# A four-layer graph network on one core: attention rows ahead of copies, a bias added in pieces, and the order of work at the changes of layer

## The chip, the cores and the metric

The kernel runs on one core of a Trainium2 chip. Its engines are named as in the profile: PE (TensorE, matrix products; PEld is its weight load), DVE (VectorE), ACT (ScalarE), POOL (GpSimd) and SP (SyncE, which issues the transfers). Each engine has one queue and works it off in order. The metric is the time of one execution on the device, in microseconds (us), and the median over runs is compared. The clock that PE was granted is given as a share of full speed.

## The reference

The input is `x` [32, 512, 128] (32 batches of 512 nodes with 128 features, f32) and one adjacency matrix `adj` [512, 512] with positive weights where there is an edge. Four layers follow, each of the form x = x + layer(h) with h = relu(layernorm(x)):

- layer 0: A is a softmax over the rows of a score matrix that stands only on the edges; out = diag(A) h W0 + (A without its diagonal) h W1 + bias
- layer 1: the polynomials x1 = adj^T h and x2 = 2 adj^T x1 - h, and then relu([h, x1, x2, x1, x2] Theta + bias); the kernel has x2 from one matrix ("cheb", 2 adj adj - 1) that is made once
- layer 2: f = relu(h psi + psi_b); m = (adj*adj)^T f; out = relu([m, h] phi1 + phi1_b) phi2 + phi2_b
- layer 3: scores (h q)(h k)^T / sqrt(128), then 8 tanh(./8), exp, a mask by adj, rows divided by their sum, and the product with h and v

## The kernel before

**Pairs and stages.** The 32 batches are worked on in 16 pairs, q = 0 to 15; a pair's `x` stays in SBUF as `xt[q]`, 128 partitions by 1024 elements, from its load to its store. Each layer is a generator (`layer0` to `layer3`), whose `yield`s cut it into stages. At the end of the kernel a loop with the lists `waiting` and `active` runs them: in each step it starts the generators of one entry of `waiting`, and takes every active one to its next `yield`. So layer 1 of pair 15 and layer 2 of pair 0 are active together, and so on. After the prologue a scheduler orders the instructions of each engine from the sequence in which they were written; an instruction that is wrapped in `keep_in_program_order` is not moved ahead of what is written before it.

**The prologue** (up to line 614) is written in the order in which it is to run. It makes the attention matrix of layer 0 in four row blocks: `score_rows` on PE, `softmax_rows` (L553 to L557, DVE and ACT), `scaled_rows` (L561 to L566; ACT multiplies, POOL takes the diagonal off), and `transpose_rows` (L403, PE), whose four banks `p_attT` are copied to `attT` at L598. In between stand the pieces of work of the first pairs: `normal` (relu and normalising, L216 on ACT), `turned` (PE transposes L248 and the copy L251 on ACT), `project` (p_g, L365, and its copy L397), and `pieces[i]`, the rows of the cheb matrix (L414). `p_adiag` (L606) and layer 0's products `p_l` wait for the whole of `attT`.

**Products by seven.** Products with the 512x512 matrices are made for two batches together with seven products of half-size blocks instead of eight (`mixed` and `products`, L299 to L350). Their right sides come from `right_blocks`: four POOL operations, L290 to L293, named rt_h or rt_feat. The results gather in the PSUM banks a, c and d, in the sequence

```
ORDER = ((1, "a", True), (6, "c", True), (5, "d", True), (7, "c", False), (2, "a", False),
         (4, "c", False), (3, "d", False))
```

Between two products in bank c, DVE takes the first one out: L332 evicts product 6, and product 7 then goes on in the same bank.

**Layer 1** ends with L709 (y on DVE) and L710, x = max(y, 0) + x, which has two inputs in SBUF. **Layer 2** evicts f on DVE (L723) and takes its relu on ACT (L724), makes rt_feat on POOL, forms msgT (L312), adds phi2_b to the whole pair in one POOL operation (L730), goes through phi1 (L735, L736) and phi2, and adds the result to x (L741). `ln_stats` then has the statistics of the next layer: L194 (DVE), L200 (ACT), L203 and L205 (DVE). **Layer 3** normalises on DVE with eight operations of 128x128 (L229, SBUF to SBUF), turns h with DVE's 32x32 transposes (L258, hb) and a bounce through DRAM, makes scores (L765), tanh (L766) and exp (L768) on ACT, the mask in turns on DVE and POOL (L770), av (L777), the sum into x (L782), and stores 256 KB for each batch (L784).

Of the kernel before, what the change touches and what calls it, by code (L numbers as in the profile page):

```python
# [15 lines left out]
P = 128  # L16
# [8 lines left out]
def kernel(  # L25
# [37 lines left out]
    nc = tc.nc  # L63
    B, N, D = x.shape
# [41 lines left out]
    xt = []  # L106
# [17 lines left out]
    def spread(w, n):  # L124
        return w[:, None, :].to_broadcast([P, n, D])
# [274 lines left out]
    def transpose_rows(banks, src, t):  # L400

        for j in range(NT):
            nc.tensor.transpose(banks[j][:, blk(t)], src[:, t, blk(j)], ident)  # L403
# [156 lines left out]
    def scaled_rows(t, u):  # L560
        nc.vector.reciprocal(total[:, t : t + 1], total[:, t : t + 1])  # L561
        nc.scalar.mul(split(att[:, t, :]), crossed(u), total[:, t : t + 1])
        own = split(att[:, t, :])[:, :, t, :]
        d = diag[:, t, :].rearrange("p (b c) -> p b c", c=QR)
        nc.gpsimd.tensor_mul(d, own, ident.rearrange("p (b c) -> p b c", c=QR))
        nc.gpsimd.tensor_sub(own, own, d)  # L566
# [8 lines left out]
    pt = [bank(f"p_attT_{j}") for j in range(NT)]  # L575
    us = []
    for t in range(NT):
        if t == NT - 1:
            next(project[0], None)
        us.append(softmax_rows(t))  # L580
        if t == 0:
            next(ln[1], None)
        else:
            scaled_rows(t - 1, us[t - 1])
        for _ in range(3):
            next(normal[1], None)
    scaled_rows(NT - 1, us[-1])
    next(turned[1])
    for t in range(NT):
        transpose_rows(pt, att, t)  # L590
    next(turned[1], None)
    nc.scalar.copy(qk, p[:, :D])
    rights = {0: right_of(0)}
    next(project[1])
    for q in (2, 3):
        next(ln[q])
    for j in range(NT):
        (nc.vector.tensor_copy if j % 2 else nc.scalar.copy)(attT[:, j, :], pt[j])  # L598
    next(project[1], None)
    for _ in sum_steps(attT, "att", nc.vector):  # L600
        pass
# [6 lines left out]
    for q in (2, 3):  # L608
        next(ln[q])
        next(ln[q], None)  # L610
    for i in (2, 3):
        for _ in pieces[i]:
            pass
    by_source.__exit__(None, None, None)


# [75 lines left out]
    def layer1(q):  # L692
        h = normed(q)
        yield
        hT = transposed(h, f"hT1_{q}")
        right = right_blocks(lambda J, b: h[:, b, 2 * J : 2 * J + 2, :], f"h_{q}", [nc.gpsimd] * 4)
        yield
        x1T = pair_tile(f"x1T_{q}").rearrange("p (b w) -> p b w", b=2)
        x2T = pair_tile(f"x2T_{q}").rearrange("p (b w) -> p b w", b=2)
        mixes = (mixed(f"x1T_{q}", sums["adj"], right, x1T), mixed(f"x2T_{q}", sums["cheb"], right, x2T))  # L700
        for _ in zip(*mixes):
            pass
        hs = [straight(hT, b, None, f"hs_{q}_{b}") for b in range(2)]
        yield
        for b in range(2):
            po = projected(f"p_l1_{q}_{b}", (columns(hs[b]), th[:, 0, :]), (columns(x1T[:, b]), th12[:, 0, :]),
                           (columns(x2T[:, b]), th12[:, 1, :]))
            y = late.tile([P, NT, D], F32, tag="y", name=f"y1_{q}_{b}", bufs=2)
            nc.vector.tensor_add(y, po, spread(b1, NT))  # L709
            nc.vector.scalar_tensor_tensor(xt[q][:, b], y, 0.0, xt[q][:, b], OP.max, OP.add)  # L710
        ln_stats(q)

    def layer2(q):
        h = normed(q)
        yield
        hT = transposed(h, f"hT2_{q}")
        yield
        yield
        feat = []
        for b in range(2):  # L720
            pf = projected(f"p_feat_{q}_{b}", (at(hT, b), psi))
            feat.append(late.tile([P, NT, D], F32, tag="y", name=f"feat_{q}_{b}", bufs=2))
            nc.vector.tensor_add(feat[b], pf, spread(psib, NT))  # L723
            nc.scalar.activation(feat[b], feat[b], AF.Relu)  # L724
        yield
        right = right_blocks(lambda J, b: feat[b][:, 2 * J : 2 * J + 2, :], f"feat_{q}", [nc.gpsimd] * 4)
        msgT = pair_tile(f"msgT_{q}").rearrange("p (b w) -> p b w", b=2)
        for _ in mixed(f"msgT_{q}", sums["sq"], right, msgT):
            pass
        nc.gpsimd.tensor_add(xt[q], xt[q], phi2b[:, None, None, :].to_broadcast([P, 2, NT, D]))  # L730
        yield
        h1T = pair_tile(f"h1T_{q}").rearrange("p (b w) -> p b w", b=2)
        for b in range(2):
            ph = bank(f"p_phi1_{q}_{b}")
            nc.tensor.matmul(ph, phi1[:, 1, :], hT[:, :, b, :], start=True, stop=False)  # L735
            nc.tensor.matmul(ph, phi1[:, 0, :], msgT[:, b], start=False, stop=True)  # L736
            nc.scalar.activation(crossed(h1T[:, b]), split(ph), AF.Relu, bias=phi1b)  # L737
        yield
        for b in range(2):
            po = projected(f"p_l2_{q}_{b}", (columns(h1T[:, b]), phi2))  # L740
            nc.vector.tensor_add(xt[q][:, b], po, xt[q][:, b])  # L741
        ln_stats(q)

    def layer3(q):
        h = normed(q, on_act=False)
        yield
        hT = transposed(h, f"hT3_{q}")
        yield
        yield
        for b in range(2):  # L750
            pp = bank(f"p_qkh_{q}_{b}")
            nc.tensor.matmul(pp, qk, hT[:, :, b, :], start=True, stop=True)  # L752
            both = work.tile([P, 2 * N + 2 * NT], F32, tag="pair", name=f"qkh_hv_{q}_{b}", bufs=5)
            qkh = both[:, :N]
            nc.vector.tensor_copy(crossed(qkh), split(pp))

            pv = projected(f"p_hv_{q}_{b}", (at(hT, b), vw))
            hv = both[:, N : N + NT * (D + 1)].rearrange("p (t f) -> p t f", f=D + 1)
            nc.gpsimd.memset(hv[:, :, D : D + 1], 1.0)
            nc.vector.tensor_copy(hv[:, :, :D], pv)  # L760
            yield
            ex = square_tile(f"ex_{q}_{b}")
            for t in range(NT):
                ps = bank(f"p_score_{q}_{b}_{t}")
                nc.tensor.matmul(ps, hT[:, t, b, :], qkh, start=True, stop=True)  # L765
                nc.scalar.activation(ex[:, t, :], ps, AF.Tanh, scale=1.0 / (8.0 * math.sqrt(D)))  # L766
            for t in range(NT):
                nc.scalar.activation(ex[:, t, :], ex[:, t, :], AF.Exp, scale=8.0)  # L768
                eng = nc.gpsimd if t % 2 else nc.vector
                eng.tensor_mul(ex[:, t, :], ex[:, t, :], adjTx[0][:, t, :])  # L770
            yield
            rsum = stats.tile([P, NT], F32, tag="rsum", name=f"rsum_{q}_{b}", bufs=4)
            for i0 in range(0, NT, 2):
                po = bank(f"p_av_{q}_{b}_{i0}").rearrange("p (i f) -> p i f", i=2)
                for i in range(2):
                    for t in range(NT):
                        nc.tensor.matmul(po[:, i, : D + 1], ex[:, t, blk(i0 + i)], hv[:, t, :],  # L777
                                         start=(t == 0), stop=(t == NT - 1))
                nc.vector.reciprocal(rsum[:, i0 : i0 + 2], po[:, :, D])
                for i in range(2):  # L780
                    xi = xt[q][:, b, i0 + i, :]
                    nc.vector.scalar_tensor_tensor(xi, po[:, i, :D], rsum[:, i0 + i : i0 + i + 1], xi,  # L782
                                                   OP.mult, OP.add)
            nc.sync.dma_start(out[2 * q + b].rearrange("(t p) f -> p t f", p=P), xt[q][:, b])  # L784

    adjTx = []

    def square():

        sq = square_tile("sq")  # L790
        load_crossed(sq, adj)
        adjTx.append(square_tile("adjTx"))
        load_crossed(adjTx[0], adjT_d)
        yield
        for i in range(NT):
            s = late.tile([P, N], F32, tag="hs", name=f"sq_{i}", bufs=2)
            nc.gpsimd.tensor_mul(split(s), crossed(sq[:, i, :]), crossed(sq[:, i, :]))
            nc.gpsimd.tensor_copy(sq[:, i, :], s)
        yield from sum_steps(sq, "sq")
# [10 lines left out]
    for q in range(2, NQ):  # L810
        waiting[max(q - 4, 0)].append(first[q])
    waiting[3].append(late_sums())
    waiting += [[layer1(q)] for q in range(NQ)]
    waiting[NQ + 6].append(square())
    for layer in (layer2, layer3):
        waiting += [[layer(q)] for q in range(NQ)]
    active = []
    while waiting or active:
        if waiting:
            active += waiting.pop(0)  # L820
        active = [g for g in active if next(g, active) is not active]


# [30 lines left out]
```

## Time and profile before

The median of three runs is 998.81 us (998.48 to 999.64). The profiled execution has a span of 998.5 us at a mean granted clock of 0.993.

| engine | busy us | share |
|---|---|---|
| PE | 976.4 | 98% |
| DVE | 630.4 | 63% |
| ACT | 440.9 | 44% |
| POOL | 395.1 | 40% |

PE's waits lie at these places:

| us | what PE waits for | idle us |
|---|---|---|
| 0 to 5 | the transfer of adj | 4.2 |
| 34 to 38 | transposes of h and the attention rows, prologue | 2.1, 0.3 |
| 456 | L332 late in layer 1 | 1.8 |
| 490 to 496 | L724, first pair of layer 2 | 3.5, 0.5 |
| 550 | L332 in layer 2 | 1.3 |
| 987 to 990 | L770 of the last pair | 0.9, 0.4 |

The busy time of an engine is summed over stages with different limits. PE's is so near the span that the rows of this table, with the times at which its clock falls, tell more than the busy times. In a line of a timeline, the start comes first, then the duration, engine, line, operation, out<-in, the tile's shape, the number of instructions, and in brackets how long the engine was idle before it and what released it. A group's duration runs from the start of its first to the end of its last instruction, and matmuls overlap, so that consecutive ones start before their forerunner ends.

### The profile page before, as it was taken

Reading aid. Unit: us, or ns where it says so; the run is one execution under the profiler, and the core shown is the slowest. Engines: PE = TensorE matmul, PEld = TensorE weight load, DVE = VectorE, ACT = ScalarE, POOL = GpSimd, SP = SyncE. Lnnn points to the kernel's source line nnn. Section 1 sums busy time; section 2 is a strip of 40 time slices with the busy share of each in tenths; the row PEclk is TensorE's granted clock in tenths of the full one; section 3 lists DMA queues with packets and bytes.
Section 4 is the critical chain, followed back from the end, with each engine's and each line's share of the span. In section 5 each row is a group of like instructions: output and inputs, shape, how many; then the busy total and the mean of one; then the engine's idle time right before and its main releaser. Section 6 shows DMA issues by size and latency. Waiting matters only on the chain.

```text
span 998.5 us, 16127 instructions
## 1 busy us (share of the span) xinstructions
PE 976.4 (98%) x5918; PEld 809.4 (81%) x5918; DVE 630.4 (63%) x1520; ACT 440.9 (44%) x967; POOL 395.1 (40%) x478
## 2 busy tenths in 40 slices
PE   8999999999999999999899999999999999999997
PEld 4699999989999999998777777777667777767776
DVE  8678787655555655558667888777754444444443
ACT  4863537112322323237566343333464455544452
POOL 2579998841217213136455112222132333222332
PEclk9999999999999999999899999999999999999999
DMA  9256644412131222215333344322222121211111
GB/s 254 85 134 179 179 125 130 106 52 76 43 85 43 64 64 54 73 44 140 93 94 106 102 121 122 90 71 78 69 70 74 43 74 53 72 55 54 53 30 35
DMA packets 83007, 87.17 MB, mean 87 GB/s; under 512 B 6768, under 2 KB 73072, under 8 KB 82928
## 3 DMA queue, kind: packets, MB, share of 16 engines
q1 hardware_dynamic: 82928, 86.14, 30.7%
q8 instruction: 47, 0.77, 0.3%
q14 instruction: 32, 0.26, 0.1%
HBM read 44.70 MB, written 41.42 MB: 86 GB/s over the span
## 4 chain that ended last, share of the span: by engine, by line
PE 88%; DVE 6%; ACT 2%; DMA 1%; issue 1%; POOL 1%; SPq 1%; POOLq 0%; DVEq 0%; ACTq 0%
PE p_av L777 11%; PE p_score L765 10%; PE p_l L365 10%; PE p_msgT_c L312 4%; PE p_l_c L319 4%; PE p_x1T_c L312 4%; PE p_x2T_c L312 4%; PE p_hv L365 3%; PE p_g L365 3%; PE p_msgT_a L312 3%; PE p_x1T_a L312 3%; PE p_x1T_d L312 3%; PE p_x2T_a L312 3%; PE p_x2T_d L312 3%; PE p_qkh L752 3%; PE p_l_d L319 3%
## 5 line engine op out<-in xcount | busy, mean ns | idle before, releaser
L216 ACT ACTIVATE h<-x,sh,rs 128x128 f32<-128x128 f32 x384 | 154.5, 482 | 58.4 <-PE p_x2T_d L312 46.0
L770 POOL TENSOR_TENSOR ex<-ex,adjTx 128x512 f32<-128x512 f32 x64 | 83.3, 1303 | 200.3 <-issue 147.7
L777 PEld LDWEIGHTS p_av<-qkh_hv,ex 128*128 128x128 f32 x1024 | 120.3, 193 | 11.6 <-issue 6.9
L766 ACT ACTIVATE ex<-p_score 128x512 f32<-128x512 f32 x128 | 71.8, 587 | 130.6 <-issue 112.9
L777 PE MATMUL p_av<-qkh_hv,ex 128*128 128x129 f32 x1024 | 122.9, 277 | 2.2 <-POOL ex L770 1.4
L765 PE MATMUL p_score<-qkh_hv,hT 128*128 128x512 f32 x256 | 115.1, 592 | 0.0
L258 DVE STREAM_TRANSPOSE hb_hT<-h 128x512 f32<-128x512 f32 x122 | 84.8, 701 | 24.5 <-ACT h L216 23.9
L194 DVE BATCH_NORM_STATS2 bn<-x 128x6 f32<-128x256 f32 x256 | 95.1, 419 | 1.9
L770 DVE TENSOR_TENSOR ex<-ex,adjTx 128x512 f32<-128x512 f32 x64 | 45.9, 717 | 76.1 <-ACT ex L768 76.1
L765 PEld LDWEIGHTS p_score<-qkh_hv,hT 128*128 128x128 f32 x256 | 46.2, 190 | 46.4 <-issue 44.2
L768 ACT ACTIVATE ex<-ex 128x512 f32<-128x512 f32 x128 | 76.5, 630 | 1.9
L290 POOL TENSOR_TENSOR rt_h<-h 128x256 f32<-128x256 f32 x16 | 11.6, 727 | 133.9 <-PE p_x2T_c L312 133.1
L290 POOL TENSOR_TENSOR rt_feat<-feat,feat 128x256 f32<-128x256 f32 x16 | 11.6, 726 | 126.3 <-ACT feat L724 126.3
L730 POOL TENSOR_TENSOR x<-x,phi2b 128x1024 f32<-128x1024 f32 x16 | 38.0, 2375 | 33.2 <-ACT h L216 33.2
L365 PE MATMUL p_l<-th,x2T 128*128 128x128 f32 x256 | 49.5, 275 | 0.0
L365 PE MATMUL p_l<-th,x1T 128*128 128x128 f32 x256 | 49.5, 275 | 0.0
L365 PE MATMUL p_l<-th,hs 128*128 128x128 f32 x256 | 49.5, 275 | 0.0
L397 ACT COPY g<-p_g 128x512 f32<-128x512 f32 x32 | 18.3, 579 | 62.4 <-PE p_g L365 62.3
L365 PEld LDWEIGHTS p_hv<-vw,hT 128*128 128x128 f32 x256 | 33.6, 192 | 14.9 <-issue 7.9
L634 POOL TENSOR_TENSOR hd<-hT,adiag 128x512 f32<-128x512 f32 x32 | 40.3, 1273 | 7.1 <-PE p_l_e L655 2.5
L737 ACT ACTIVATE h1T<-p_phi,phi1b 128x512 f32<-128x512 f32 x32 | 21.9, 686 | 44.9 <-PE p_phi L736 44.9
L365 PEld LDWEIGHTS p_l<-th,hs 128*128 128x128 f32 x256 | 40.1, 192 | 0.8
(229 smaller groups left out, 2181.0 us busy)
## 6 DMA issues: line engine op xcount, KB each, us to landing
d_hT<-hb_hT SPq DMA_DIRECT2D x244, 128.0 KB
hT<-d_hT SPq DMA_DIRECT2D x61, 512.0 KB
x<-in_x_dram SPq DMA_DIRECT2D x32, 256.0 KB
out_dram<-x SPq DMA_DIRECT2D x32, 256.0 KB
adj_s<-in_adj_dram SPq DMA_DIRECT2D x4, 256.0 KB
adjT_d<-adjT SPq DMA_DIRECT2D x1, 1024.0 KB
sq<-in_adj_dram SPq DMA_DIRECT2D x4, 256.0 KB
adjTx<-adjT_d SPq DMA_DIRECT2D x4, 256.0 KB
```

The lines of the kernel that those rows point to most:

```text
L194: ins = nc.vector.bn_stats(st[:, k].rearrange("p e s -> p (e s)"), xt[q][:, b, t : t + 2, :].rearrange("p t f -> p f t"))
L216: nc.scalar.activation(h[:, b, t, :], xt[q][:, b, t, :], AF.Relu, bias=shift[q][:, i : i + 1], scale=scale[q][:, i : i + 1])
L258: nc.vector.transpose(hb[:, :, b].rearrange("p j t r -> p t j r"), h[:, b].rearrange("p t (j c) -> p t j c", c=QR))
L312: nc.tensor.matmul(p[:, :H], b[:, k, :], a[:, k, :], start=(first and k == 0), stop=(k == 1), skip_group_check=True)
L319: nc.tensor.matmul(p[:, i * D : (i + 1) * D], a[:, k, blk(i)], b[:, k, :], start=(first and i == 0 and k == 0), stop=(k == 1), skip_group_ ...
L365: nc.tensor.matmul(p[:, blk(t)], hT(t), w, start=(i == 0), stop=(i == len(terms) - 1))
L634: nc.gpsimd.tensor_mul(split(s), src, split(scale))
L765: nc.tensor.matmul(ps, hT[:, t, b, :], qkh, start=True, stop=True)
L766: nc.scalar.activation(ex[:, t, :], ps, AF.Tanh, scale=1.0 / (8.0 * math.sqrt(D)))
L768: nc.scalar.activation(ex[:, t, :], ex[:, t, :], AF.Exp, scale=8.0)
L770: eng.tensor_mul(ex[:, t, :], ex[:, t, :], adjTx[0][:, t, :])
L777: nc.tensor.matmul(po[:, i, : D + 1], ex[:, t, blk(i0 + i)], hv[:, t, :], start=(t == 0), stop=(t == NT - 1))
```

## The change

Four things are changed:

1. In the prologue, two of pair 1's relu operations instead of three follow each softmax row on ACT, none follows the last, and the copies of p_g come after the last softmax. The transposes of attention rows 0 and 1 and one row of cheb are put on PE ahead of rows 2 and 3, and pair 1's h is turned later. The aim is that PE has work while the last rows of the softmax are made.
2. phi2_b is added in four POOL operations of 128x256 per pair, each held to program order, instead of one of 128x1024. It is to keep POOL from doing it early, and to have it hold what it shares with others for less time at once.
3. `layer1(0)` starts in the step of the last pair of layer 0, and `layer2(0)` in that of the last pair of layer 1, ahead of it in the list; all later pairs follow one step sooner. `square()`, which makes adj*adj, keeps its place relative to layer 1. The first pair of a layer is to be ready when the last of the layer before is done.
4. When only two generators are left, the list is turned round once, so that the last scores of pair 15 come ahead of the last av of pair 14; and the last batch is stored in two halves.

```diff
     for t in range(NT):
-        if t == NT - 1:
-            next(project[0], None)
         us.append(softmax_rows(t))
         if t == 0:
             next(ln[1], None)
         else:
             scaled_rows(t - 1, us[t - 1])
-        for _ in range(3):
-            next(normal[1], None)
+        if t < NT - 1:
+            for _ in range(2):
+                next(normal[1])
+        if t == 2:
+            transpose_rows(pt, att, 0)
+            transpose_rows(pt, att, 1)
+            next(pieces[2])
+            next(pieces[2])
     scaled_rows(NT - 1, us[-1])
+    next(project[0], None)
+    for _ in normal[1]:
+        pass
+    transpose_rows(pt, att, 2)
+    transpose_rows(pt, att, 3)
     next(turned[1])
-    for t in range(NT):
-        transpose_rows(pt, att, t)
-    next(turned[1], None)
-    nc.scalar.copy(qk, p[:, :D])
     rights = {0: right_of(0)}
-    next(project[1])
...
         (nc.vector.tensor_copy if j % 2 else nc.scalar.copy)(attT[:, j, :], pt[j])
+    next(turned[1], None)
+    next(project[1])
+    nc.scalar.copy(qk, p[:, :D])
+    next(pieces[2], None)
     next(project[1], None)
...
-        nc.gpsimd.tensor_add(xt[q], xt[q], phi2b[:, None, None, :].to_broadcast([P, 2, NT, D]))
+        for b in range(2):
+            for i in range(0, NT, 2):
+                xi = xt[q][:, b, i : i + 2, :]
+                tc.keep_in_program_order(nc.gpsimd.tensor_add(xi, xi, spread(phi2b, 2)))
...
+                if b == 1 and q == NQ - 1:
+                    nc.sync.dma_start(out_r[:, i0 : i0 + 2, :], xt[q][:, b, i0 : i0 + 2, :])
+            if not (b == 1 and q == NQ - 1):
+                nc.sync.dma_start(out_r, xt[q][:, b])
...
-    waiting += [[layer1(q)] for q in range(NQ)]
-    waiting[NQ + 6].append(square())
-    for layer in (layer2, layer3):
-        waiting += [[layer(q)] for q in range(NQ)]
+
+    waiting[-1].insert(0, layer1(0))
+    waiting += [[layer1(q)] for q in range(1, NQ)]
+    waiting[NQ + 5].append(square())
+    waiting[-1].insert(0, layer2(0))
+    waiting += [[layer2(q)] for q in range(1, NQ)]
+    waiting += [[layer3(q)] for q in range(NQ)]
     active = []
     while waiting or active:
         if waiting:
             active += waiting.pop(0)
+        if not waiting and len(active) == 2:
+            active.reverse()
         active = [g for g in active if next(g, active) is not active]
```

## The prediction

> **What bounds the kernel now.** I read the page's busy times and slices first, to know the bounding engine, and then TensorE's list of waits and the timelines round each wait.
>
> ```profile
> PE 976.4 (98%) x5918; PEld 809.4 (81%) x5918; DVE 630.4 (63%) x1520; ACT 440.9 (44%) x967; POOL 395.1 (40%) x478
> PEclk9999999999999999999899999999999999999999
> ```
>
> TensorE (PE) is busy for 976.4 of 998.5 us, so only about 22 us are idle and a shorter time must come out of these, or out of stretches at a lower clock. The one 8 in the clock row is a slice near 490 us. The waits of PE, as total, number, longest:
>
> ```profile
> PE p_msgT_a L312 <- ACT feat L724: 3.5, 1, 3.5
> PE p_attT L403 <- ACT hT L251: 2.1, 1, 2.1
> PE p_x1T_c L312 <- DVE u_x1T L332: 1.8, 1, 1.8
> PE p_msgT_c L312 <- DVE u_msgT L332: 1.5, 2, 1.3
> PE p_av L777 <- POOL ex L770: 1.4, 2, 0.9
> ```
>
> Each happens once or twice, at a change of stage. Two cost more than their length, as the timeline of PE shows (start, duration, then the wait in brackets):
>
> ```profile
> 36.54 0.66 PE L403 MATMUL p_attT<-ident,att 128*128 128x128 f32 x4 [2.10 <-ACT hT L251]
> 37.98 3.25 PE L365 MATMUL p_g<-w,hT 128*128 128x128 f32 x16
> ...
> 487.62 1.95 PE L365 MATMUL p_feat<-psi,hT 128*128 128x128 f32 x16
> 493.08 2.07 PE L312 MATMUL p_msgT_a<-sq,feat 128*128 128x256 f32 x4 [3.51 <-ACT feat L724]
> ...
> 990.20 4.14 PE L777 MATMUL p_av<-qkh_hv,ex 128*128 128x129 f32 x20 [0.42 <-POOL ex L770]
> ```
>
> Sixteen 128x128 products take 1.95 us at 487.62 and 3.25 at 37.98; the same form at 695.26 takes 1.03 for what takes 2.07 at 493.08. After a gap PE runs for some us at half rate.
>
> In the steady part of layer 2 the queue of PE has no gap at all: from 682 to 708 us it is busy 26.0 of 26.0. What DVE and POOL do there decides what an added POOL operation costs:
>
> ```profile
> 693.91 0.73 POOL L293 TENSOR_TENSOR rt_feat<-feat,rt_feat 128x256 f32<-128x256 f32 x1
> 694.89 0.17 DVE L205 SCALAR_TENSOR_TENSOR sh<-bn,rs 128x8 f32<-128x8 f32 x1
> 695.10 2.14 DVE L229 TENSOR_SCALAR h<-x,rs,sh 128x128 f32<-128x128 f32 x8
> 697.16 0.70 DVE L258 STREAM_TRANSPOSE hb_hT<-h 128x512 f32<-128x512 f32 x1
> 697.78 0.38 DVE L332 TENSOR_TENSOR u_msgT<-p_msgT_c,u_msgT 128x256 f32<-128x256 f32 x1
> 698.28 1.08 PE L312 MATMUL p_msgT_c<-sq,rt_feat 128*128 128x256 f32 x4
> ```
>
> L332 empties the bank that the next c product fills. It ends at 698.16 and the product starts at 698.28: no slack.
>
> **What the Trainium skill says.** "SBUF — State Buffer", section "Who interferes with whom": VectorE and GpSimd share a port pair as an exclusive lock; a VectorE operation with two SBUF inputs, or one in a two-port mode, contends with a GpSimd operation that reads SBUF, and whichever issues first blocks the other fully. "VectorE: DVE Perf Modes", section "What auto-detection actually checks": a single-source operation from SBUF to SBUF can enter a two-port mode; L229 is of that kind. The trace agrees on both. L710, with two SBUF inputs, takes 0.65 us alone and 2.32 behind L730; L229, whose starts are otherwise 0.26 apart, takes 1.35:
>
> ```profile
> 448.83 2.36 POOL L730 TENSOR_TENSOR x<-x,phi2b 128x1024 f32<-128x1024 f32 x1 [0.46 <-ACT h L216]
> 449.42 2.32 DVE L710 SCALAR_TENSOR_TENSOR x<-y,x 128x512 f32<-128x512 f32 x1
> ...
> 546.22 2.36 POOL L730 TENSOR_TENSOR x<-x,phi2b 128x1024 f32<-128x1024 f32 x1
> 547.32 1.35 DVE L229 TENSOR_SCALAR h<-x,rs,sh 128x128 f32<-128x128 f32 x1
> ```
>
> "TensorE: Matmul & The Clock Gate", section "Part 1: The HAM clock gate (the "warmup" mystery)", has the clock fall to half after an idle window of about 3.4 us. The trace shows the half rate, but here a gap of 2.10 was enough once, while the one of 1.80 at 456 us was not.
>
> **The change part by part.**
>
> *Prologue.* Gone are the 2.10 and 0.29 gaps, and with them the half rate: p_g loses 3.25 - 1.95 = 1.3 to it, p_adiag (1.43 us) about 0.5. Together 4.2. The chebyshev row that now runs between the attention transposes (half of the 7.03 us of the two rows at 42.29) fills the time in which the last softmax row is made. Added: hT's copy on ACT follows the copies of attT, so p_g waits for it. By laying the ACT copies end to end (0.5 each) I get 0.85. Gain 3.3; bounds 1.5, if two more copies lie in the way, and 4.2.
>
> *phi2b in pieces, what it removes.* The single operation could run as soon as x was ready, and POOL ran it in idle spots of late layer 1 and early layer 2, ahead of need. There it blocked L710 and L229, which gave the waits of 1.8 (456 us) and 1.29 + 0.26 (550 and 565 us). Held to program order, the pieces come after rt_feat of their own pair. Gain 1.8 + 1.6 = 3.4.
>
> *What it adds.* Four operations of 128x256 per pair; one such takes 0.73 and back to back they start 0.68 apart, so 2.8 us from the end of rt_feat, against 2.36 before. POOL has the time. But rt_feat ends at 694.64 and L205 starts at 694.89, eight L229 behind it: the new lock falls exactly on these. If DVE waits once and then keeps the ports, the delay is 694.64 + 0.70 - 694.89 = 0.45. If the two alternate, L205 and three L229 wait for one piece each: the fourth piece ends about 697.7, five more L229 of 0.26 follow, and the last ends at 699.1 where it ended at 697.24: 1.9. The trace has a short case for the second: between two rt_feat operations at 573.85 and 574.65 one L229 came through and the next waited again. I take 1.4, near the upper end, since this alternation is seen over only a few operations. Queued behind the L229s is L332, and PE's c product waits for it. With PE full, all of it is lost: 8 x 1.4 = 11.2 in pairs 8 to 15. In pairs 4 to 7 the L229s stand partly behind L332; I take 1.0 each, 4.0. Pairs 0 to 3 have no L229 there and lose nothing to speak of. Loss 15.2 (bounds 5.4 and 19.7, with 0.45 for twelve pairs, or 1.9 for eight and 4.5 for four).
>
> *First pairs one step sooner.* Between layers 0 and 1 the orders of POOL and DVE hardly change and I count nothing: the 0.8 us gap at 200 us has DVE's L205 behind a POOL operation, which stays. Between layers 1 and 2, p_feat of pair 0 now stands ahead of pair 15's p_l, whose 24 products cover ACT's relu and POOL's sums. Gone are 3.51 + 0.46 idle, and some 3.0 at the low clock (the clock was 0.74 and 0.58 of full in the windows 490:495 and 495:500, and p_msgT_a took 2.07 and 2.08 for 1.03). Against 7.0 stands one new wait: DVE has y, x and the statistics of pair 15 ahead of the second feat, some 4 us of work, and pair 1's c product waits for that; estimate 1.2, between 0 and 3. Gain 5.8.
>
> *Tail.* With pair 15's last scores ahead of pair 14's last av, tanh, exp and mask lie beside 3.6 us of av. PE then runs 3.60 of scores and 3.58 of av after 983.26 without a stop and ends at 990.4, not 994.34: 3.9. The two half stores: DVE ends at 995.2 and the span at 998.5, so a whole 256 KB store takes 3.3; I put half of its data time at 0.5. Gain 4.4.
>
> Sum: 3.3 + 3.4 + 5.8 + 4.4 = 16.9 gained, 15.2 lost, net 1.7: 998.8 - 1.7 = 997.1.
>
> **The rivals.** *DVE keeps the ports once it has them:* loss 5.4, time 998.8 - 16.9 + 5.4 = 987.3. For it: eight L229 issue without a pause. Against: the case at 574 us. *No collision to speak of:* the shift of layer 2 moves rt_feat or L205 by half a us and the pieces meet transposes and statistics, which POOL did not slow anywhere in the trace: 998.8 - 16.9 = 981.9. For it: 0.25 us decides the order. Against: both hang on the same PE work, in the same order as before, and the pieces last longer than DVE's free time. *Strict alternation:* loss 19.7, time 1001.6, slower than before; with gains at their low ends 1004. For it: rt_feat and L229 at 574 us, and no slack in PE. Against: some of the delay may fall in time where the next L332 has slack.
>
> **How the numbers follow.** Forecast 0.40, DVE keeping the ports 0.20, no collision 0.14, strict alternation 0.26. The forecast lies at the bound of the 0.2% (996.8), so I halve it: 0.20 faster, 0.20 same. Strict alternation gives 0.20 slower and 0.06 same. Faster 0.54, same 0.26, slower 0.20. The range from 984 to 1003 leaves out most of the no-collision case below and the worst of the last above.
>
> **What would show it.** Right: in the stretch from 600 to 700 us, L229 in groups with a mean well over 0.27, behind pieces of phi2b, and a wait of p_msgT_c for L332 in most pairs, 1.0 to 1.9 each; no wait of p_x1T_c over 1; p_msgT_a's 3.5 gone; full clock after 990. Wrong: p_msgT_c's waits under 3 us in all, so that the time is under 990; or new waits of p_l_a after the prologue, or of pair 1's c product over 3 us, so that gains are missing.

## The result, and the profile after

The changed kernel takes 1003.51 us in the median of four runs, against 999.22 beside it on the same chip: 1.0042 of the time before, 95% interval 1.0024 to 1.0059, so 2.4 to 5.9 us slower. 997.1 had been forecast, in a range that ended at 1003. The profiled executions, which all readings below are from, have spans of 1001.6 and 998.5 us, 3.1 apart. A span is some 1.8 us shorter than the time of the same execution (1001.6 and 1003.46, 998.5 and 1000.32).

The page of the changed kernel, engines and granted clock:

```profile
PE 973.5 (97%) x5918; PEld 804.5 (80%) x5918; DVE 637.2 (64%) x1520; ACT 440.6 (44%) x967; POOL 399.4 (40%) x526
PEclk9999999999999999999999999999999999999999
```

The 8 in the clock row is gone, DVE is busy 6.8 us longer with the same 1520 instructions, so some of them take longer, and PE does the same 5918 products in a longer span, though it is busy 2.9 us less. The waits of PE say where:

```profile
PE p_msgT_c L312 <- DVE u_msgT L332: 7.7, 12, 1.6
PE p_msgT_a L312 <- ACT u_msgT L330: 5.4, 8, 0.7
PE p_adjT L403 <- DMA adj_s<-in_adj_dram: 4.0, 2, 3.6
PE p_l_c L319 <- DVE u_l L674: 2.7, 3, 1.5
PE p_g L365 <- DMA hT<-d_hT: 1.4, 1, 1.4
PE p_msgT_c L312 <- POOL rt_feat L291: 1.4, 1, 1.4
```

The waits of 3.5, 2.1 and 1.8 us are gone. Two kinds that came twice and once before now come 12 and 8 times, once in each of layer 2's pairs from 4 on or from 8 on. Two more lie in layer 0: that for the transfer of hT is new, and the longest for u_l has grown from 0.8 to 1.5.

Laying the start of the same PE work in the two timelines side by side gives a balance by stretch; each row is the difference over that stretch alone (after minus before, us):

| stretch | forecast | measured |
|---|---|---|
| to the first p_l_a of layer 0 (49.2, 45.7 us) | -3.3 | -3.4 |
| the rest of layer 0 | 0 | +3.0 |
| layer 1 to its end | -1.8 | -2.1 |
| change to layer 2, to p_feat of pair 4 (540.5, 531.9) | -5.8 | -6.0 |
| layer 2, to the first p_qkh (699.6, 706.9) | -1.6 + 15.2 | +15.7 |
| layer 3, to the scores of the last batch but one | 0 | 0 |
| the end | -4.4 | -4.1 |
| sum | -1.7 | +3.1 |

Two rows are off: layer 0, where the prologue's gain does not last, and layer 2, which costs 2.1 more than forecast.

**Layer 2.** A late pair in the timelines of POOL, DVE, ACT and PE of the changed kernel (from layer 0 on, line numbers are 7 to 11 higher than before; L740 are the pieces):

```profile
684.87 0.73 POOL L293 TENSOR_TENSOR rt_feat<-feat,rt_feat 128x256 f32<-128x256 f32 x1
685.55 2.79 POOL L740 TENSOR_TENSOR x<-x,phi2b 128x256 f32<-128x256 f32 x4
```

```profile
685.85 0.46 DVE L205 SCALAR_TENSOR_TENSOR sh<-bn,rs 128x8 f32<-128x8 f32 x1
686.34 3.37 DVE L229 TENSOR_SCALAR h<-x,rs,sh 128x128 f32<-128x128 f32 x8
689.63 0.70 DVE L258 STREAM_TRANSPOSE hb_hT<-h 128x512 f32<-128x512 f32 x1
690.26 0.38 DVE L332 TENSOR_TENSOR u_msgT<-p_msgT_c,u_msgT 128x256 f32<-128x256 f32 x1
```

```profile
688.71 0.63 ACT L231 ACTIVATE h<-h 128x512 f32<-128x512 f32 x1 [1.61 <-DVE h L229]
689.25 0.35 ACT L330 COPY u_msgT<-p_msgT_a 128x256 f32<-128x256 f32 x1
```

```profile
687.94 1.03 PE L312 MATMUL p_msgT_d<-sums_sq,rt_feat 128*128 128x256 f32 x4
689.66 0.70 PE L312 MATMUL p_msgT_a<-sq,feat 128*128 128x256 f32 x2 [0.69 <-ACT u_msgT L330]
690.69 1.13 PE L312 MATMUL p_msgT_c<-sq,rt_feat 128*128 128x256 f32 x4 [0.33 <-DVE u_msgT L332]
```

The same two places in the kernel before, on ACT and PE, without a wait:

```profile
696.25 0.63 ACT L231 ACTIVATE h<-h 128x512 f32<-128x512 f32 x1
697.85 0.59 PE L312 MATMUL p_msgT_a<-sq,feat 128*128 128x256 f32 x2
```

The four pieces end at 688.34. One by one, L205 ends at 686.30 and three L229 at 687.05, 687.74 and 688.42: each just after one piece (686.28, 686.97, 687.65, 688.34). This is the strict alternation of the last rival. The pieces themselves are not held up: four take 2.79 us. The eight L229 take 3.37 in place of 2.14. The delay goes to PE in two ways. L332 waits in DVE's queue, as foretold; but before that, ACT's relu L231 waits for the fourth L229, and L330, which empties bank a for PE, stands behind L231. PE stops twice, for 0.69 and 0.33. That sums to 1.0, yet a pair takes 14.8 us (p_feat at 662.5 and 677.3) where it took 13.3. The rest is hidden in the stops: groups of four products in a row start 0.86 apart but show 1.03, so each stop also loses 0.17 of overlap, and the first group after one is longer (0.70 for 0.59, 1.13 for 1.08).

**Layer 0.** PE reaches it 3.4 us sooner and then waits for what did not come sooner, or even came later:

```profile
66.54 2.02 PE L365 MATMUL p_g<-w,hT 128*128 128x128 f32 x16 [1.41 <-DMA hT<-d_hT]
...
82.58 1.16 PE L319 MATMUL p_l_c<-rt_g,attT 128*128 128x128 f32 x8 [1.51 <-DVE u_l L674]
```

The first is pair 4's h, turned through DRAM. DVE turns the second half of it, and SyncE then issues the writes and, once they have landed, the read. In the kernel before and in the changed one:

```profile
52.56 0.71 DVE L258 STREAM_TRANSPOSE hb_hT<-h 128x512 f32<-128x512 f32 x1 [0.45 <-ACT h L216]
57.79 0.34 SPq L265 DMA_DIRECT2D hT<-d_hT  x1
```

```profile
55.25 0.70 DVE L258 STREAM_TRANSPOSE hb_hT<-h 128x512 f32<-128x512 f32 x1
61.65 0.34 SPq L265 DMA_DIRECT2D hT<-d_hT  x1
```

DVE comes to the second half 2.7 us later, because the evictions of PE's earlier products and their statistics (51.16 to 55.34 us) now stand ahead of it. The read is 3.9 us later, since two writes of the next pair, for which DVE has the data at 60.66, now stand ahead of it in SyncE's queue too.

For the second wait, the timelines of POOL and DVE in the changed kernel:

```profile
78.47 2.49 POOL L641 TENSOR_TENSOR hd<-hT,adiag 128x512 f32<-128x512 f32 x2
80.92 0.71 POOL L290 TENSOR_TENSOR rt_g<-g 128x256 f32<-128x256 f32 x1
```

```profile
80.38 1.28 DVE L205 SCALAR_TENSOR_TENSOR sh<-bn,rs 128x8 f32<-128x8 f32 x2
81.58 0.41 DVE L671 TENSOR_TENSOR u_l<-p_l_a,b 128x256 f32<-128x256 f32 x1
82.10 0.42 DVE L674 TENSOR_TENSOR u_l<-p_l_c,u_l 128x256 f32<-128x256 f32 x1
```

Two L205 stand behind two POOL operations, as the pieces' L205 do, and u_l behind them. In the kernel before they take 0.28:

```profile
80.95 0.28 DVE L205 SCALAR_TENSOR_TENSOR sh<-bn,rs 128x8 f32<-128x8 f32 x2
```

Ahead of them, at 75 to 79 us, DVE also waits for three of POOL's additions into x, for 0.9, 0.5 and 0.3, where before it had not waited for POOL. So both POOL's queue and the lock are in this wait; which of the two matters more was not separated. A table by windows of the kernel before could have said so (window, then busy us of PE, PEld, DVE, ACT and POOL):

```profile
65.00:92.00 27.00, 27.00 (x244) 27.00 (x243) 22.79 (x64) 13.49 (x35) 26.06 (x32) 1.00 0.67 190
```

POOL was busy 26.06 of 27.00 us there, which left it less than 1 us to spare.

### The profile page after: what moved, and what is told of

The parts are those of the page before. It is cut to its first block, busy times and chain, and to the rows that moved or that the text cites. A ratio compares the mean times of both kernels' runs of the same rounds, so it can differ in the third digit from the quotient of the medians.

```text
span 1001.6 us, 16153 instructions
## 1 busy us (share of the span) xinstructions
PE 973.5 (97%) x5918; PEld 804.5 (80%) x5918; DVE 637.2 (64%) x1520; ACT 440.6 (44%) x967; POOL 399.4 (40%) x526
## 4 chain that ended last, share of the span: by engine, by line
PE 84%; DVE 9%; ACT 3%; issue 1%; POOL 1%; DMA 1%; SPq 0%; DVEq 0%; ACTq 0%; POOLq 0%
PE p_av L788 11%; PE p_score L775 11%; PE p_l L365 11%; PE p_x1T_c L312 4%; PE p_x2T_c L312 4%; PE p_l_c L319 4%; PE p_msgT_c L312 3%; PE p_x1T_a L312 3%; PE p_hv L365 3%; PE p_x2T_d L312 3%; PE p_x2T_a L312 3%; PE p_x1T_d L312 3%; PE p_qkh L762 3%; DVE h L229 3%; PE p_feat L365 2%; PE p_l_a L319 2%
## 5 line engine op out<-in xcount | busy, mean ns | idle before, releaser
L788 PE MATMUL p_av<-qkh_hv,ex 128*128 128x129 f32 x1024 | 120.3, 275 | 0.8 <-POOL qkh_hv L769 0.6
L229 DVE TENSOR_SCALAR h<-x,rs,sh 128x128 f32<-128x128 f32 x128 | 49.5, 450 | 0.4
L740 POOL TENSOR_TENSOR x<-x,phi2b 128x256 f32<-128x256 f32 x64 | 44.5, 728 | 0.0
L312 PE MATMUL p_msgT_c<-sq,rt_feat 128*128 128x256 f32 x128 | 34.7, 394 | 7.7 <-DVE u_msgT L332 7.7
L747 ACT ACTIVATE h1T<-p_phi,phi1b 128x512 f32<-128x512 f32 x32 | 22.0, 686 | 45.7 <-PE p_phi L746 45.7
```

What stands on the lines that cost most here:

```text
L229: nc.vector.tensor_scalar(h[:, b, t, :], xt[q][:, b, t, :], scale[q][:, i : i + 1], shift[q][:, i : i + 1], OP.mult, OP.add)
L312: nc.tensor.matmul(p[:, :H], b[:, k, :], a[:, k, :], start=(first and k == 0), stop=(k == 1), skip_group_check=True)
```

## The experiments

All times are medians, and ratios are against the kernel before on the same chip.

**Without the pieces, and with the pieces alone.** The whole operation back in the changed kernel, and the four pieces in the kernel before:

```diff
-                tc.keep_in_program_order(nc.gpsimd.tensor_add(xi, xi, spread(phi2b, 2)))
+        nc.gpsimd.tensor_add(xt[q], xt[q], phi2b[:, None, None, :].to_broadcast([P, 2, NT, D]))
```

> The changed kernel, with phi2_b in one operation of 128x1024 again, free to run early. Theory (the pieces hold the ports that L205 and L229 want, pair after pair): layer 2 has 13.28 us a pair again, and only the early operation's own waits (2.0 at the end of layer 1, 1.5 in layer 2) come back: 986 to 991 us. Rival (the step by which layer 2 was moved made it slower, the pieces are innocent): 1001 or more.

> The kernel before, with the pieces alone. Theory: 3.5 us of waits go, some 17 come in layer 2: 1010 to 1015 us. Rival (the pieces are innocent): 995 to 997.

Measured: 989.60 us (0.9899, 0.9884 to 0.9914) without them, 1007.88 (1.0085, 1.0070 to 1.0100) with them alone. So the pieces are the loss; the moved layers are innocent. Alone they cost less than expected: in that trace layer 2 lost 16.0 us from pair 4 on, but pairs 0 and 1 gained 4.2 (p_feat of pair 1 is 6.7 us earlier than before, that of pair 0 only 2.5), where the wait of 3.5 us for feat is 1.0 in this trace. Part of what was put down to the earlier start comes with the pieces too. In the kernel before, L710 of the last pair of layer 1 takes 2.83 and 1.65 us behind POOL's early operations (0.69 each with the pieces alone), and the eviction of feat stands behind it in DVE's queue.

Without the pieces only part of the expected waits came back. That of 1.80 for L332 at 456 us did; in layer 2, PE waits for L332 only once in that trace, for 0.2. The same holds for the earlier layers alone, below. So the waits of 1.29 and 0.26 in layer 2 go with the earlier start, not with the pieces.

**The same pieces at another time.** A copy of one column makes POOL wait for msgT, which ACT writes after DVE's L332:

```diff
+        gate = stats.tile([P, 1], F32, tag="gate", name=f"gate_{q}", bufs=2)
+        tc.keep_in_program_order(nc.gpsimd.tensor_copy(gate, msgT[:, 0, :1]))
         for b in range(2):
             for i in range(0, NT, 2):
```

> The changed kernel; ahead of each pair's pieces POOL copies one column of msgT, which ACT writes after DVE's L332, so that the same pieces run some 5 us later, beside transposes and evictions. Orders of PE, DVE and ACT are those of the changed kernel. Theory (the place alone counts): the loss in layer 2 goes, all gains stay: 983 to 987 us. Rival (POOL's work or the holding of the order is what costs): 1000 to 1004.

Measured: 986.43 us (0.9868, 0.9853 to 0.9883). PE, DVE and ACT run all their operations in the same order as in the changed kernel. POOL and DVE of a late pair in this kernel:

```profile
671.64 0.72 POOL L293 TENSOR_TENSOR rt_feat<-feat,rt_feat 128x256 f32<-128x256 f32 x1
677.98 0.18 POOL L738 COPY gate<-msgT 128x1 f32<-128x1 f32 x1 [5.62 <-ACT msgT L338]
678.12 2.78 POOL L742 TENSOR_TENSOR x<-x,phi2b 128x256 f32<-128x256 f32 x4
```

```profile
672.83 2.14 DVE L229 TENSOR_SCALAR h<-x,rs,sh 128x128 f32<-128x128 f32 x8
...
678.83 0.42 DVE L340 TENSOR_TENSOR msgT<-p_msgT_c,u_msgT 128x256 f32<-128x256 f32 x1 [0.83 <-PE p_msgT_c L312]
```

POOL does the same work in the same 2.78 us, but starts it 6.5 us after the start of L293 where the changed kernel has 0.7, beside DVE operations with one input in PSUM, and none of these is longer (L340 takes 0.42 in the kernel before too). The eight L229 are back at 2.14. Place alone makes some 17 us (1.0042 to 0.9868 of the time before). It is also 3.2 us better than the whole operation left free to run early (989.6 to 986.4, on the same chip). Against this trace, the changed kernel loses 4.6 us in pairs 4 to 7 and 12.0 in pairs 8 to 15, 1.5 in each.

**One operation in the place of the four.** Held to program order, not cut:

```diff
+        tc.keep_in_program_order(
+            nc.gpsimd.tensor_add(xt[q], xt[q], phi2b[:, None, None, :].to_broadcast([P, 2, NT, D])))
```

> The changed kernel, with one operation of 128x1024 held to program order in place of the four. Theory (a lock for the whole of an operation): no L229 gets through until it ends at 2.36 us, so the last ends some 0.5 us later than between the pieces; 12 pairs make 1006 to 1010 us. Rival (each change of hands between POOL and DVE costs time of its own, so that four are dearer than one): 996 to 1001.

Measured: 1011.32 us (1.0117, 1.0100 to 1.0134), 1.3 us above what was expected at most. A late pair, POOL and then DVE:

```profile
692.82 2.36 POOL L738 TENSOR_TENSOR x<-x,phi2b 128x1024 f32<-128x1024 f32 x1
```

```profile
693.11 2.09 DVE L205 SCALAR_TENSOR_TENSOR sh<-bn,rs 128x8 f32<-128x8 f32 x1
695.24 2.14 DVE L229 TENSOR_SCALAR h<-x,rs,sh 128x128 f32<-128x128 f32 x8
```

L205, alone 0.17 us, is held for the rest of POOL's operation, and all eight L229 follow it undisturbed. That is the exclusive lock that the Trainium skill states ("SBUF — State Buffer", section "Who interferes with whom"), for the whole of one instruction. A pair takes 15.2 us (14.8 with the pieces), which is 1.9 over the 13.3 of before, and in two of the earlier pairs waits of 2.15 and 2.06 us are followed by the slow clock (PE at half rate), which the pieces avoid; that accounts for the time above what was expected. The cut does what it was made for: it lets one DVE operation through after each piece, and is worth about 7.5 us here (1.0117 to 1.0042 of the time before). Of the difference between the two traces, 3.3 lie in pairs 8 to 15, 0.4 in each, and 5.3 in pairs 4 to 7, with the slow clock in them. But the program order that came with it put the pieces in the worst place.

**Where the prologue's gain went.** The old prologue in the changed kernel, and the new one in the kernel before:

> The changed kernel with the prologue of before. Theory (the prologue's gain of 3.9 us at the start of layer 0 is handed back by two waits in layer 0, for the transfer of hT at 65 us and for POOL's chain at 81 us, so it is worth 0.5 at the end of layer 0): 1003 to 1005 us. Rival (the two waits come from other parts of the change, and the prologue's gain is whole): 1006 to 1008.

> The kernel before with the new prologue alone. Theory: 998 to 999.2 us (0.5 gained), with the two waits of layer 0 in the trace. Rival: 995 to 996.

Measured: 1003.60 us (1.0053, 1.0032 to 1.0073) and 998.25 us (1.0001, 0.9991 to 1.0012). As it stands, the new prologue is worth nothing. The trace of the second starts layer 0 3.2 us sooner than before, has waits of 1.06 for hT and 1.51 for u_l, and leaves layer 0 0.2 sooner.

This does not rest on two traces. From the first p_l_a to the first product of layer 1, the six traces of all the runs that have the new prologue and leave POOL's sums where they were take 160.2 to 160.6 us, and the five with the old prologue 157.3 to 157.8. The two waits share the loss differently each time: hT takes 0.90 to 2.79, and where it takes 1.99 or more there is none for u_l.

**The earlier layers and the end, each alone in the kernel before.**

> The kernel before with layers 1 and 2 one step sooner, nothing else. Theory: 6 us gained between layers 1 and 2, nothing between 0 and 1: 992 to 994 us. Rival (part of the 6 us was the pieces' doing, since POOL is free of the early operations there): 995 to 997.

> The kernel before with the list turned round for the last two generators, and the last store whole. Theory: 3.9 us from the order, nothing or up to 0.5 missing for the store: 995 to 996 us. Rival (the halved store is the larger part of the tail's 4.1): 997.5 or more.

Measured: 993.47 us (0.9962, 0.9945 to 0.9978), in its trace 6.3 us between the last x1T of layer 1 and p_feat of pair 5 (6.0 in the whole change); and 995.58 us (0.9970, 0.9960 to 0.9979), in its trace 3.7 at the end. In the traces both gains are close to the forecast; by time they come out smaller, at 2.2 to 5.5 us for the earlier layers and 2.1 to 4.0 for the end (the intervals). The halved store was not run alone; beside the 4.1 of the whole change, this trace leaves some 0.4 for it.

The 6.3 has two parts. Up to p_feat of pair 4, where the forecast of 5.8 ends, it is 4.9, as in the trace without the pieces; the other 1.4 is the wait for L332 that layer 2 no longer has. In the whole change the 6.0 up to pair 4 is thus some 4.9 from the earlier start and 1.0 from the pieces.

**Freeing POOL in layer 0.** On top of the gated pieces, the sums that POOL makes for layer 1 start three steps later:

```diff
-    waiting[3].append(late_sums())
+    waiting[6].append(late_sums())
```

> The changed kernel with gated pieces, and the eight POOL operations that make the sums for layer 1 (L283, 1.27 us each) start three steps later in layer 0. Theory (POOL, busy 26 of 27 us between 65 and 92 us in the kernel before, is what takes the prologue's gain back at 81 us): the wait of p_l_c for u_l of 1.6 us goes, 984.5 to 985.5 us. Rival (it comes back wherever the sums are put, since POOL is 87% busy all through layer 0): 986 to 987, with the wait some steps later.

Measured: 985.84 us (0.9873, 0.9854 to 0.9891). The wait of 1.65 for u_l at 81 us is gone from the trace and does not come back later. The rest of layer 0 takes 158.4 us, and 158.8 in the repeat below, in place of 160.2 to 160.6. By time alone this could not be told from the gated pieces on another chip, so both were run again, side by side, with a third that has the old prologue:

> Gated pieces and late sums once more, on the chip of the run beside it: 984.5 to 986 us.

> The gated pieces with the sums where the change has them, once more: 1.0 to 1.6 us above the run with late sums if the removed wait of 1.6 us is a gain in time, the same if it is not.

> Gated pieces and late sums, loads where they were, the prologue of before. If POOL's sums were what took back the larger part of the prologue's gain, this is 1.5 to 2.5 us slower than the same kernel with the new prologue. Rival (the transfer of hT alone bounds the start of layer 0): the same within 0.7.

Measured: 984.94 us with late sums (0.9869, 0.9854 to 0.9883), 986.07 with the sums where they were, 986.78 with late sums and the old prologue. With POOL freed the prologue is worth 1.8 us and the later sums 1.1; the intervals of the three (each about 1.5 us to either side) overlap, so the traces have to carry it. Layer 0 is left 2.5 us sooner than before with both, 0.2 with the sums where they were, 0.1 with the old prologue. But the trace with the sums where they were lost its gain in another way than before:

```profile
67.01 3.49 PE L365 MATMUL p_g<-w,hT 128*128 128x128 f32 x16 [1.99 <-DMA hT<-d_hT]
```

Its wait for hT is 1.99, not 0.90 as in the first run of the same kernel, and the slow clock follows (3.49 us for about 2); PE is then late enough to meet no wait for u_l. The read was issued 0.3 us sooner than in that first run (61.51 and 61.84) and PE's product starts 0.8 later, so the transfer itself varies from run to run, and POOL is the second bound behind it. That late sums take away POOL's wait is shown; that they save 1.1 us in the median is not beyond the intervals.

**The transfer of hT.** Loads of x for later pairs started two steps later still, and then the old prologue with that:

```diff
-        waiting[q - NQ // 2].append(loads(q))
+        waiting[q - NQ // 2 + 2].append(loads(q))
```

> As the run before, and the loads of x for pairs 8 to 15 start two steps later. Theory (they share the transfer engines with the bounce of hT for pair 4): the wait of p_g for the transfer, 0.9 us, goes too: 983.5 to 984.5 us. Rival (the bounce is late because DVE and ACT are, not the transfers): no change from the run before.

> As the run before, with the prologue of the kernel before. If the prologue's gain was only taken back by POOL and transfers, it is now 3 to 4 us against the run before: 987 to 988 us. Rival (something else takes it back): the same as the run before within 1 us.

Measured: 987.50 us (0.9889, 0.9873 to 0.9906) and 986.42 (0.9880, 0.9865 to 0.9895). A miss: the wait did not go.

```profile
67.44 3.09 PE L365 MATMUL p_g<-w,hT 128*128 128x128 f32 x16 [2.39 <-DMA hT<-d_hT]
70.33 1.66 PE L319 MATMUL p_l_a<-g,attT 128*128 128x128 f32 x8
```

It is 2.39 here, where it was 1.24 and 1.74 in the two runs with late sums alone, and after it PE runs slow again, 3.09 us for what takes about 2. So this pair of runs could not show what the prologue is worth: the new one lost 4 us to a wait, and the slow clock after it, that the old one, later there, did not meet. The read of hT was issued at 61.54 (60.77 in the run before, whose start was 0.78 earlier), so neither DVE nor ACT was later than in that run. What made the transfer itself longer is open: from the issue of the read to PE's product it is 4.4 to 6.3 us in the nine traces with the new prologue, and the longest, with a wait of 2.79, has the loads where they were. So one trace does not show that later loads made it worse, only that the theory's 0 was not reached. The rival, that DVE is late, holds for part of it: in all nine the read is issued at 60.6 to 61.9 us, and in the kernel before at 57.8.

## Why the prediction was wrong, point by point

- *Prologue, gain 3.3.* This is the step that failed, with 2.8 of the 4.8 us that the forecast missed in the spans. Up to the first p_l_a it was right in size (3.4); of its terms, the wait for hT's copy is 0.45 in place of 0.85, and 0.25 of the 0.29 stays. The half rate that it counted is not met in every execution of the old prologue: two of the seven traces that have it are free of it and start layer 0 at 47.3 us, the others at 48.7 to 49.4; the nine with the new one start it at 44.7 to 46.0. But the prediction took the start of layer 0 as the end of the path. It put new waits of p_l_a after the prologue among its signs of being wrong, but counted nothing for what the faster PE would meet next. PE met the transfer of hT (1.41), whose read comes 3.9 later, and POOL's queue (1.51); 0.5 was left in this trace, and nothing in the time of either run that changes only the prologue. With POOL's sums out of the way 1.8 came back (986.8 to 984.9, intervals overlapping).
- *phi2b in pieces, what it removes, 3.4.* Half right. The 456 us wait is gone (2.1 over layer 1). The 1.6 in layer 2 is gone too, but it goes with the earlier start of layer 2 alone, as the two runs without pieces show, so it was put down to the wrong part; and with gated pieces the stretch from pair 4 on is only 0.8 shorter than before.
- *What it adds, 15.2.* This is the second step that was off. The mechanism, the place and the pairs were right, the size was too small: the traces show 12.0 + 4.6 = 16.6, and with 0.8 in place of 1.6 for what the pieces remove, that is the 2.1 that layer 2 cost more. The term of 1.4 measured 1.5, that of 1.0 measured 1.15. The forecast lay between "once" and "strict alternation"; strict alternation is what happens. Its own 1.9 was too much, since it let each piece be late by some 0.1 for the DVE operation between; the pieces kept their spacing and ended 2.7 us after rt_feat, not 3.1. The way by ACT (L231 ahead of L330) was not seen at all. That the 1.4 came so near to 1.5 is therefore in part luck.
- *First pairs one step sooner, 5.8.* Right in size (6.0), in part by luck, since the earlier start alone makes 4.9 of it. The new wait is there, 1.41 for 1.2, though its releaser is rt_feat behind ACT's relu rather than an eviction; DVE's work ahead of the second feat is the reason, as stated. Nothing was gained between layers 0 and 1, also as stated: the wait at 200 us is 0.81 and 0.82.
- *Tail, 4.4.* 4.1.
- *The rivals.* "No collision" and "DVE keeps the ports" fall with the alternation; "strict alternation" at 1001.6 was the true course in layer 2, and with the prologue at its due, the span before gives 998.5 - 13.6 - 0.5 + 16.6 = 1001.0, where the changed kernel's is 1001.6. The time went 0.5 beyond the range's upper end: the range gave the prologue's low end at 1.5, where it should have been zero. The 1004 named for strict alternation with low gains is too low as well: with 1.5 for the prologue and 3 for the new wait, the prediction's own terms give 1001.6 + 1.8 + 1.8 = 1005.2.

As they stand, two of the four parts are worth keeping, the earlier layers and the end. The pieces pay once they stand behind a gate, and the prologue only if POOL's sums move, as far as the times can tell. With the pieces behind a gate and the sums three steps later, the kernel takes 0.9869 of the time before (0.9854 to 0.9883), about 13 us less, and beats both.

## What to carry to other kernels

When an edit lets the bounding engine reach a stage sooner, ask before counting the gain which other engine is nearly full in that stage, which a table of busy times by windows shows, and which transfers have their source made by an engine that the earlier work will keep busy. An operation with no dependency, held to program order, runs as soon as the one ahead of it is done; if it must stay clear of another engine, give it something to wait for. Cutting a POOL operation lets DVE through after each piece, but here it was free only where DVE had none of the kinds that were held: L205 and L710 with two SBUF inputs, and the scaling L229 from SBUF to SBUF.

## What the runs showed of the hardware that was not expected

- Where four POOL operations follow each other and DVE has a queue of L229, the two take strict turns: one DVE operation after each piece, and POOL loses nothing (2.79 us for four, 2.78 when DVE is elsewhere). DVE bears the whole cost.
- The listed waits of PE understate what a stop costs: 1.0 us of them made a pair 1.5 longer, 0.17 of it for the lost overlap of each stop. (The profile models the ends of products; the 1.5 is read from starts.)
- The length of a wait does not decide alone whether the slow clock follows. Waits for hT or L332 of 1.99, 2.06, 2.15 and 2.39 us brought it (3.09 us for about 2 of work after 2.39), those of 1.3 to 1.65 in the changed kernel did not. But a wait of 2.79, in the run without pieces, did not either; and PE's wait of 2.1 in the old prologue brought it in five of the seven traces that have it, and not in two. The first line is from the run without pieces, the second from the run with the old prologue, where the kernel before takes 3.25:

```profile
66.85 2.02 PE L365 MATMUL p_g<-w,hT 128*128 128x128 f32 x16 [2.79 <-DMA hT<-d_hT]
37.70 1.95 PE L365 MATMUL p_g<-w,hT 128*128 128x128 f32 x16
```

  The Trainium skill ("TensorE: Matmul & The Clock Gate", section "Part 1: The HAM clock gate (the "warmup" mystery)") speaks of an idle window of about 3.4 us; here less was enough at times. What decides it is open.
- The same kernel's time goes with the granted clock of the execution: of 29 runs of the kernel before on one chip, the seven at 0.992 or 0.993 took 998.9 to 1000.9 us and the three at 0.998 took 995.1 to 996.3. The profile that the prediction read was at 0.993. That may be why gains read from it are larger than those by time; this was not tested.
